# The second layer's front computed by image pairs in program order, attention's rows repeated by the transfer, and two sets of weights built beside the first layer

## Chip, core and metric

The kernel runs on one core of a Trainium2 chip. Time is device time in microseconds (us); lower is better. The kernel before takes 5074.72 us, the median of three runs (5069.09 to 5077.64). The profiled execution is a further run, of 5081.34 us; every position in the text, such as "at 4302.1", is a time in us from the start of its span of 5079.4 us.

The engines are TensorE (PE; its weight loads are shown as PEld), VectorE (DVE), ScalarE (ACT), GpSimd (POOL) and SyncE (SP). SP and ACT issue the transfers (DMA).

## What is computed

The input x has 4 images of 48 x 48 positions with 128 channels, in fp32. There are two layers, each of the form x + f(group_norm(x)).

- Layer 0 is a state-space block: projection to 256 channels, a 3 x 3 convolution, and four scans over the 2304 positions (rows and columns, both ways) with 16 states each; then a normalisation, a gate and a projection back.
- Layer 1 takes the result as 4 sequences of T = 48 frames, each frame a plane of H = 48 by W = 128. It is cut here to what the text needs:

```python
xa_n = inorm(x.reshape(B * T, 1, H, W))           # each frame normalised over its plane
q, k, v = (fno(xa_n, w, ws) for w, ws in (Q, K, V))   # 32 heads each
scores = einsum('bhtd,bhsd->bhts', q, k) / sqrt(d)
out = einsum('bhts,bhsd->bhtd', softmax(scores), v)
attention = inorm(fno(out, wP, wPs) + x)
m = fno(fno(inorm(attention), wM0), wM1)          # with norms and gelu
result = inorm(m) + attention
```

Here `fno(x, w, ws)` is a product by complex weights on the low frequencies of the plane's two-dimensional Fourier transform, transformed back, plus a scaled copy of x.

## The kernel before

**Layouts.** Channels (which are W in layer 1) lie on the 128 partitions. The first layer writes its result `x1` to DRAM as [image, 128, 48, 48]. In the second layer `xa` holds all four images as [128, H = 48, BT = 192], the 192 columns being image by frame. A *pair* is two images, 96 columns. In the second half of the layer the two pairs run as two strands.

**Layer 0 (`layer0`, L54 to 618).** For each of 4 images, 4 directions (in the order 0, 2, 1, 3), 5 chunks of 480 or 384 positions and 16 states there is one step, 1280 in all. The order is written out by hand: operations called through `on` (the class `Ordered`, L36) keep program order on their engine. In a step ACT makes the decay `da` (two activations), VectorE and GpSimd make the input `db`, VectorE runs the scan `h`, GpSimd multiplies `hc` by the row `cbc`, and PE adds up. SP fetches `cbc` and `bbc`, one DRAM row into all 128 partitions, for each group of steps (L425, L429). Work of the background is written as generators in the list `later`; `piece()` (L529) advances one of them by one `yield` per step. The generator `front` (L258) for the next image is put into `later` in the middle of an image's first direction; the last image has no such generator. `back` (L343) writes finished chunks of x1.

**Layer 1's front (`layer1`, L644 on).** Operations here that are called directly on an engine are put in order by the framework's scheduler, not by the program text. The stages are:

- `xa` is loaded from x1, one image at a time by SP and ACT in turn.
- group norm: ACT copies blocks of 8 rows (L993), VectorE takes `bn_stats` of them (L994), `group_affine` (L621) turns means and variances into a scale and a shift per channel and image, and four VectorE operations apply it to `xa` (L1000).
- `first_norm` (L696): the mean of each frame by 48 matmuls with a matrix `mean_m` of constants (L700), subtraction by VectorE and GpSimd (L707), squares by ACT (L709), their mean by another 48 matmuls (L711), and the reciprocal root r.
- `spectral_weights` (L949 to 980): the MLP's two sets of weights are put between Fourier matrices. GpSimd scales `ih` by a weight into `wih` (L972), PE multiplies (L977), ACT copies the result into `spw`, a single buffer (L979), and SP stores it to `sp_d` (L980). There are 16 rounds.
- `prepare` (L824 to 947): selection matrices, and the Q and K weights read with about 140 small transfers each set into its place, and their products `g_qk`.
- V and P weights: their products `gw`, transposed by PE, copied by ACT to `gtt` (L791), and stored by SP to `dgt` (L792) with each of 32 heads repeated 16 times.
- `forward_w` (L722): the transform along W by 48 matmuls (L730); VectorE multiplies by r while it evacuates PSUM (L731), SP stores to `da_x` (L734), and `load_a2` (L737) reads it back turned as `a2`.
- 96 transposes `pxn` (L1024) and their scaled copies `xnt` by ACT (L1027), and 192 matmuls `psel` that select rows of the spectrum (L1042).
- `gp_qk` is a copy of `g_qk` (L1109); with it the scores start.

**Attention.** Scores, softmax and the transposed weights `attn_c` come from L1110 to 1168. Then follow constants `wpv` and `mask` (L1194 to 1203) and the chunk loop (L1220 to 1277): 2 pairs x 4 k x 3 q = 24 steps. In each, `xrep` (1.18 MB, rows of `dxt` repeated 8 times) is loaded with 16 transfers of 16 rows (L1228). At q = 0, four `grep` tiles of 128 rows are loaded from `dgt` (L1236). ACT copies part of `grep` to `gp` (L1243), VectorE multiplies `v` (L1245), GpSimd multiplies `v3` (L1249), and 48 matmuls per step add to `acc` (L1253). At the end of each k the sums become `zt`, which PE transposes as `pz` (L1264 to 1274).

**The rest.** `Strand` has phases p0 to p5 (L1342 to 1700) for the projection back, the norms and the MLP, with the weights `sp_m` read from `sp_d`.

Transfers that SP or ACT issues take one of eight completions per queue in rotation, so that a transfer waits until the one eight places before it in its queue has landed.

Of the kernel before, what the change touches and what calls it, by code (L numbers as in the profile page):

```python
# [53 lines left out]
def layer0(ctx, tc, io, x1_dram):  # L54
# [8 lines left out]
    const = ctx.enter_context(tc.tile_pool(name="l0_const", bufs=1))  # L63
    one = ctx.enter_context(tc.tile_pool(name="l0_one", bufs=1))
# [4 lines left out]
    small = ctx.enter_context(tc.tile_pool(name="l0_small", bufs=2))  # L69
    ps_s = ctx.enter_context(tc.tile_pool(name="l0_pss", bufs=1, space=PSUM))  # L70
    ps_b = ctx.enter_context(tc.tile_pool(name="l0_psb", bufs=1, space=PSUM))
    ps_a = ctx.enter_context(tc.tile_pool(name="l0_psa", bufs=1, space=PSUM))
# [207 lines left out]

    def load_dt(b, k):
        w_dt = two.tile([32 + R, D], F32, tag="w_dt", name=f"w_dt{b}_{k}")
        nc.sync.dma_start(w_dt[32 : 32 + R], io["dt_proj_wT"][k])
        return w_dt
# [58 lines left out]
    def back(b, s, n, yb, x, w, wb):  # L343
# [46 lines left out]
        nc.sync.dma_start(x1_dram[b].rearrange("w h t -> w (h t)")[:, s : s + n], xo[:, 0:n])  # L390
# [196 lines left out]
    for j, chunks in enumerate(directions):  # L587
# [9 lines left out]
        for m, c in enumerate(chunks):  # L597
            c.carry = carries[j % 2]
            for i in range(N):
                if k == ORDER[0] and b + 1 < B and m > 1 and coming is None and not any(g in later for g in backs):  # L600
                    coming = front(b + 1, images[b + 1])
                    later.append(coming)
                if i in (N // 2 + 3, N // 2 + 6):
# [13 lines left out]
    while later:  # L617
        piece()

# [24 lines left out]
def layer1(ctx, tc, io, x1_dram, out):  # L644
# [5 lines left out]
    nc = tc.nc  # L650
    img = ctx.enter_context(tc.tile_pool(name="l1_img", bufs=1))
    const = ctx.enter_context(tc.tile_pool(name="l1_const", bufs=1))
    small = ctx.enter_context(tc.tile_pool(name="l1_small", bufs=2))
    dram = ctx.enter_context(tc.tile_pool(name="l1_dram", bufs=1, space=DRAM))
    dmas = [nc.sync, nc.scalar]
# [6 lines left out]
    def everywhere(name, src, n):  # L662
        return load(name, [128, n], src.partition_broadcast(128), nc.scalar)

    ident = load("ident1", [128, 128], io["c_ident"])
    gmat = load("gmat1", [128, 128], io["c_group"])
    fw = load("fw", [128, 66], io["c_FW"])
    fh = load("fh", [96, 96], io["c_FH"])
    fhi = load("fhi", [96, 96], io["c_FHI"])
    ih = load("ih", [96, 96], io["c_IH"])  # L670
    eps = const.tile([128, 1], F32, name="eps1")
    nc.gpsimd.memset(eps, 1e-5)
    mean_m = const.tile([128, 128], F32, name="mean_m")
    nc.gpsimd.memset(mean_m, 1.0 / (H * W))
    n_g = everywhere("n_g", io["L1_norm_g"], 6)
# [3 lines left out]

    turn = [0]  # L680

    def either():
        turn[0] += 1
        return nc.gpsimd if turn[0] % 3 == 0 else nc.vector
# [8 lines left out]
    def per_image(t, n=HB):  # L693
        return t[:, None, :].to_broadcast([128, n, BT])

    def first_norm(psum, work, x):  # L696

        pm = psum.tile([128, 512], F32, tag="st", name="pm_in")
        for q in range(H // 2):
            nc.tensor.matmul(pm[:, 0 : 2 * BT], mean_m, x[:, 2 * q : 2 * q + 2], start=(q == 0), stop=(q == H // 2 - 1))  # L700
        m = small.tile([128, BT], F32, tag="in_m", name="in_m")
        nc.scalar.copy(m, pm[:, 0:BT])
        nc.vector.tensor_add(m, m, pm[:, BT : 2 * BT])
        pv = psum.tile([128, 512], F32, tag="st", name="pv_in")
        for q in range(0, H, HB):
            d = x[:, q : q + HB]
            either().tensor_sub(d, d, per_image(m))  # L707
            sq = work.tile([128, HB, BT], F32, tag="blk", name=f"sq_{q}")
            nc.scalar.activation(sq, d, AF.Square)  # L709
            for j in range(0, HB, 2):  # L710
                nc.tensor.matmul(  # L711
                    pv[:, 0 : 2 * BT], mean_m, sq[:, j : j + 2], start=(q + j == 0), stop=(q + j == H - 2)
                )
        r = small.tile([128, BT], F32, tag="in_r", name="in_r")
        nc.scalar.copy(r, pv[:, 0:BT])
        nc.vector.tensor_add(r, r, pv[:, BT : 2 * BT])
        nc.scalar.activation(r, r, AF.Sqrt, bias=eps)
        nc.vector.reciprocal(r, r)
        nc.vector.tensor_scalar(r, r, n_g[:, 0:1], None, ALU.mult)
        return r  # L720

    def forward_w(psum, work, src, r, name):  # L722


        da = dram.tile([2, 33, H, BT], F32, name=f"da_{name}")
        for q in range(0, H, HB):
            a = work.tile([66, HB, BT], F32, tag="blk", name=f"a_{name}{q}")
            for j in range(0, HB, 2):
                p = psum.tile([128, 512], F32, tag="mm", name=f"pa_{name}{q}_{j}")
                nc.tensor.matmul(p[0:66, 0 : 2 * BT], fw, src[:, q + j : q + j + 2], start=True, stop=True)  # L730
                nc.vector.tensor_mul(  # L731
                    a[:, j : j + 2], p[0:66, 0 : 2 * BT].rearrange("p (a t) -> p a t", t=BT), per_image(r, 2)[0:66]
                )
            nc.sync.dma_start(da.rearrange("c k h t -> (c k) h t")[:, q : q + HB], a)  # L734
        return da

    def load_a2(a2, da, n):  # L737
        for c in range(2):
            for i, s in enumerate(range(0, n, 11)):
                e = min(s + 11, n)  # L740
                dmas[i % 2].dma_start(a2[c * 48 : (c + 1) * 48, s:e], da[c, s:e].rearrange("k h t -> h k t"))

    xa = img.tile([128, H, BT], F32, name="xa")
    for b in range(B):
        dmas[b % 2].dma_start(xa[:, :, b * T : (b + 1) * T], x1_dram[b])

    pair_t = [img.tile([128, H, 128], F32, tag=f"p{p}", name=f"xnt{p}") for p in range(2)]
    sp_d = [dram.tile([96, 32, 96], F32, name=f"sp_d{i}") for i in range(2)]
# [4 lines left out]
    dgt = dram.tile([4, NH, 16, 3 * NC], F32, name="dgt")  # L753
    with ExitStack() as pw:
        ps_t = pw.enter_context(tc.tile_pool(name="l1_wt", bufs=2, space=PSUM))
        q1 = pw.enter_context(tc.tile_pool(name="l1_w1", bufs=1))

        w_p = q1.tile([128, 12, 2, NH], F32, name="w_p")
        w_v = q1.tile([128, 6, 2, NH], F32, name="w_v")
        d48 = [q1.tile([128, 128], F32, name=f"d48{c}") for c in range(2)]  # L760
        for c in range(2):
            dmas[c].dma_start(w_p[:, :, c], io["wP"][c].rearrange("(j p) h -> p j h", p=128))
            dmas[c].dma_start(w_v[:, :, c], io["wV"][c].rearrange("(j p) h -> p j h", p=128))
            dmas[c].dma_start(d48[c], io[("c_D48r", "c_D48i")[c]])
        for c in range(2):
            p = ps_t.tile([128, 512], F32, tag="tr", name=f"pv48{c}")
            nc.tensor.matmul(p[:, 0:NH], d48[c], w_v[:, 0, c], start=True, stop=True)
            nc.scalar.copy(w_v[:, 0, c], p[:, 0:NH])
# [55 lines left out]
    def prepare():  # L824
# [36 lines left out]
        with ExitStack() as pw:  # L861
# [21 lines left out]
            def weights(side, name, ws, gen, zero, mirror):  # L883
# [5 lines left out]
                for c in range(2):  # L889
# [6 lines left out]
                    for o, r, m in zero:  # L896
                        nc.sync.dma_start(w[o : o + m, 0, c], row[r : r + m])
# [935 lines left out]
```

## Time and profile before

| | |
|---|---|
| median of three runs | 5074.72 us (5069.09 to 5077.64) |
| profiled execution, its span | 5081.34 us, 5079.4 us |
| busy in the span | PE 4207.3, DVE 4169.1, POOL 4034.6, ACT 2923.0 us |
| layer 0, from the start to the last add on x1 | 4200.2 us |
| from there to `gp_qk` | 206.6 us (to 4406.8) |
| scores, softmax, `wpv`, `mask`, `pa0` | to 4543.8 |
| chunk loop | to 4809.4 |
| strands' phases | from 4814.3 to the end |
| layer 0's directions in images 0 to 2 | 260.3, 240.6, 245.4, 265 us |
| the same in image 3 | 249.5, 237.3, 239.5, 262.1 us |

How to read the lines: a line of the *windows* has, for each stretch of time, the busy time and number of instructions of each engine, the granted PE clock (1.00 is full), the share of the DMA engines' time and GB/s. A line of the *chain* has the start, the length and what it was; the chain is followed back from the last instruction to what released each one. A line of the *timeline* has start, length, engine, operation, output and inputs with their shapes, the count, and in brackets the idle time before it and what ended it. A line of the *waits* has who waited for what, the total, the count and the longest.

### The profile page before, as it was taken

To read this page: it belongs to the slowest core of one execution; us is meant where nothing else is said; L and a number is where in the kernel's file an instruction comes from. 1 tells how busy PE (TensorE), PEld (TensorE's weight loads), DVE (VectorE), ACT (ScalarE), POOL (GpSimd) and SP (SyncE) were. 2 spreads that over 40 slices of the span, in tenths; PEclk is the share of its full clock that TensorE was granted. 3 is DMA by queue.
4 is the path that set the end of the run, shared out by engine and by line. 5 is a ranking of instruction groups with operands and counts; after the bars stand their busy time and mean duration, and the time that the engine had idled before them with its cause. 6 is when DMAs were issued, how large, how long until landed. Compare 5 with 4: busy or idle time off the path is not lost. (4 is left out here: it accounts for less than half of the span.)

```text
span 5079.4 us, 44364 instructions
## 1 busy us (share of the span) xinstructions
PE 4207.3 (83%) x12344; PEld 1893.5 (37%) x12344; DVE 4169.1 (82%) x2888; ACT 2923.0 (58%) x6467; POOL 4034.6 (79%) x2219
## 2 busy tenths in 40 slices
PE   6889898888798988887989888878787785888876
PEld 2334333333343333333433333333333332453343
DVE  3689998989899989898999898999999873356636
ACT  3566566666565666665656666656666652223334
POOL 4589998988899989888999898999999873246532
PEclk9989999999899999998999999999999987889977
DMA  1223232322233323222333232333332216236646
GB/s 54 73 88 101 92 114 92 101 88 98 94 106 105 106 91 101 88 98 94 106 103 107 91 102 88 97 105 106 100 103 92 97 66 131 59 82 171 162 106 153
DMA packets 276766, 509.25 MB, mean 100 GB/s; under 512 B 100602, under 2 KB 185434, under 8 KB 276326
## 3 DMA queue, kind: packets, MB, share of 16 engines
q1 hardware_dynamic: 265318, 502.61, 32.5%
q10 hardware_dynamic: 11200, 3.81, 0.5%
q8 instruction: 97, 1.59, 0.1%
q14 instruction: 151, 1.24, 0.1%
HBM read 462.58 MB, written 43.72 MB: 100 GB/s over the span
## 5 line engine op out<-in xcount | busy, mean ns | idle before, releaser
L50 POOL TENSOR_TENSOR hc<-h,cbc 128x960 f32<-128x960 f32 (+1 forms) x1280 | 2719.7, 2140 | 449.2 <-DVE h L50 338.4
L50 DVE TENSOR_TENSOR_SCAN h<-da,carry,db 128x961 f32<-128x961 f32 (+1 forms) x1280 | 2702.4, 2129 | 153.8 <-ACT carry L50 106.0
L50 ACT ACTIVATE da<-dt,a_neg 128x480 f32<-128x480 f32 (+1 forms) x2560 | 1661.3, 649 | 1233.9 <-DVE h L50 1189.3
L50 PE MATMUL yp<-hc,ident 128*128 128x480 f32 (+1 forms) x5120 | 2273.9, 572 | 6.6 <-POOL hc L50 6.4
L50 PEld LDWEIGHTS yp<-hc,ident 128*128 128x128 f32 x5120 | 1006.3, 198 | 1409.7 <-issue 1018.9
L50 DVE TENSOR_TENSOR db<-du,pb 128x960 f32<-128x960 f32 (+1 forms) x960 | 1063.8, 1108 | 232.2 <-PE pb L50 176.8
L50 POOL TENSOR_TENSOR db<-du,bbc 128x960 f32<-128x960 f32 (+1 forms) x320 | 688.6, 2152 | 0.0
L50 PE MATMUL pb<-bs,pick 112*128 112x480 bf16 (+1 forms) x960 | 359.2, 374 | 391.3 <-DVE db L50 389.9
L50 PE MATMUL pc<-pad,cdiag 128*128 128x480 f32 (+1 forms) x630 | 284.6, 564 | 9.0 <-ACT pad L50 9.0
L1249 POOL TENSOR_TENSOR v<-grep,xrep 128x768 f32<-128x768 f32 x96 | 174.1, 1820 | 115.9 <-PE acc L1253 57.7
L1253 PE MATMUL acc<-v,attn_c 128*64 128x384 f32 x1152 | 214.8, 514 | 28.0 <-POOL v L1249 17.8
L1245 DVE TENSOR_TENSOR v<-gp,xrep 128x1536 f32<-128x1536 f32 x96 | 165.1, 1754 | 86.8 <-DMA xrep<-dxt 35.2
L50 POOL TENSOR_TENSOR du<-dt,xc 128x480 f32<-128x480 f32 (+1 forms) x160 | 205.0, 1282 | 37.2 <-ACT dt L50 37.2
L50 ACT COPY db<-carry 128x1 f32<-128x1 f32 x1280 | 226.7, 177 | 7.5 <-DVE db L50 4.2
L50 PE MATMUL px<-xc,w_xp 128*112 128x480 f32 (+1 forms) x320 | 215.0, 759 | 17.0 <-ACT xc L50 13.3
L50 PEld LDWEIGHTS <-pick 112*128 112x128 bf16 x960 | 97.9, 102 | 335.4 <-issue 311.8
L50 ACT ACT_TABLE_LOAD x147 | 188.6, 1283 | 25.7 <-PE gv_g L50 13.8
L50 PE MATMUL pd<-xd,w_dt 8*128 8x480 f32 (+1 forms) x320 | 167.6, 604 | 39.3 <-ACT bs L50 24.4
L50 ACT COPY carry<-h 128x2 f32<-128x2 f32 x1024 | 193.2, 189 | 0.0
L50 PEld LDWEIGHTS pc<-pad,cdiag 128*128 128x128 f32 x630 | 122.1, 195 | 142.4 <-issue 114.7
L50 PE MATMUL yp<-y,ident 128*128 128x480 f32 (+1 forms) x240 | 164.6, 815 | 0.2
L1253 PEld LDWEIGHTS acc<-v,attn_c 128*64 128x64 f32 x1152 | 89.8, 142 | 149.2 <-issue 65.8
(366 smaller groups left out, 3128.9 us busy)
## 6 DMA issues: line engine op xcount, KB each, us to landing
cbc<-cd SPq DMA_DIRECT2D x512, 480.0 KB
bbc<-cd SPq DMA_DIRECT2D x256, 240.0 KB
cbc<-cd SPq DMA_DIRECT2D x128, 384.0 KB
xrep<-dxt SPq DMA_DIRECT2D x384, 72.0 KB
grep<-dgt SPq DMA_DIRECT2D x32, 576.0 KB
bbc<-cd SPq DMA_DIRECT2D x64, 192.0 KB
dgt<-gtt SPq DMA_DIRECT2D x4, 2304.0 KB
x<-in_xT SPq DMA_DIRECT2D x16, 288.0 KB
```

What stands on the lines that cost most here:

```text
L50: return lambda *args, **kw: self._tc.keep_in_program_order(emit(*args, **kw))
L1245: nc.vector.tensor_mul(v, gp[:, None, :, 0:NC].to_broadcast([128, 2, 2, NC]), x[:, :, 0:2])
L1249: nc.gpsimd.tensor_mul(v3, r[:, 2:3].to_broadcast([128, 2, NC]), x[:, :, 2])
L1253: nc.tensor.matmul(acc[c][64 * b : 64 * b + 64, 0:NC], attn_c[:, 2 * pair + b, g, q], v[:, b, c] if c < 2 else v3[:, b], start=first, stop ...
```

## The change

1. The first layer becomes `first_layer`, called from within `layer1`, after DRAM tiles for `sp_d`, `d_w` and `d_m` are made. In its last image a new generator, `matrices`, is put into `later` where other images have `front`. It writes the Q and K weights in their places into DRAM (`d_w`, `d_m`) by about 150 small transfers, and computes `sp_d` with ACT's scaling in place of GpSimd's, in the buffer of `cdiag`, which is idle in that image.
2. The second layer's pools of images, constants and small tiles lie on the other side of the memory. x1 is loaded by pairs into `x_in` ([128, 2, H, T]). Only the last chunk of the last image is stored and loaded by ACT's queue; all others go by SP, and come in program order ahead of it.
3. The front runs through `on`, pair by pair, with the two generators `first_norm` and `forward_w` interleaved. Statistics are taken on `x_in` directly. The group norm's scale goes into the Fourier matrix (`fwa`) and into the vectors of the means (`a_m`), its shift into small corrections. One operation normalises and subtracts the mean. The sums over frames use 32 output columns, in four column groups. r is applied to `a2` after it is loaded, and the Fourier mean is subtracted there. Evacuation goes to VectorE and ACT in turn. The products of V and P weights come after both pairs, and those of Q and K (`products`) after `a2`.
4. `dgt` has each head once. `xrep` and `grep` are filled with one transfer per image or tile that repeats its rows; partitions of `xrep`, `grep`, `attn_c`, `wpv` and `mask` are now ordered (key, head) instead of (head, key).
5. `ih` is loaded just before the strands.

The core of the diff:

```diff
+    def matrices():
+        room = one.tile([128, 9, 128], F32, tag="cdiag", name="matrices")
...
+        for of in range(2):
+            nc.sync.dma_start(
+                d_w[of].rearrange("p c j h -> p (c j) h"), zero[:, None].to_broadcast([128, 8, NH])
+            )
+            nc.sync.dma_start(d_m[of], zero[0:32, None].to_broadcast([32, 2, NH]))
+        yield FREE
...
+                for o, r, m in general + [(at_8, 8, 4)]:
+                    for j in range(4):
+                        k = int(j == 0)
+                        nc.sync.dma_start(dst[j][k:, o : o + m], src[j][k:, r : r + m])
+                    yield FREE
...
+        for n in range(2):
+            for k in range(0, 32, 2):
+                for c in range(2):
+                    for i in range(2):
+                        on.scalar.activation(m[3 + 2 * c + i], m[2], AF.Copy, scale=w[:, n, c, k + i : k + i + 1])
+                    if c == 0:
+                        yield FREE
...
+                on.scalar.copy(room[:, 7 * 96 : 9 * 96], p[0:96, 0:192])
+                nc.sync.dma_start(
+                    sp_dram[n][:, k : k + 2].rearrange("p k m -> p (k m)"), room[:, 7 * 96 : 9 * 96]
+                )
+                yield FREE
...
+                if k == ORDER[0] and b + 1 == B and m > 1 and coming is None and not any(g in later for g in backs):
+                    coming = matrices()
+                    later.append(coming)
...
+    def statistics(psum, p, x):
+        mv = small.tile([128, 2, 2], F32, tag=f"mv{p}", name=f"mv{p}", bufs=1)
+        for b in range(2):
+            st = small.tile([128, 6, 6], F32, tag="st", name=f"st1_{p}_{b}")
+            for q in range(6):
+                on.vector.bn_stats(st[:, q], x[:, b, q * HB : (q + 1) * HB].rearrange("p h t -> p (h t)"))
...
+    def forward_w(psum, work, p, x, aff):
...
+                on.tensor.matmul(pa[0:66, 0 : HB * T], fwa[:, b], x[:, b, q : q + HB], start=True, stop=True)
...
+            nc.scalar.dma_start(
+                da.rearrange("c k h t -> (c k) h t")[:, q : q + HB], a.rearrange("p h b t -> p h (b t)")
+            )
+            yield
...
+    def first_norm(psum, work, p, x, aff, y):
...
+                on.tensor.matmul(
+                    pm[32 * i : 32 * i + 32, 0 : HB * T],
+                    a_m[:, b : b + 1].to_broadcast([128, 32]),
+                    x[:, b, h + q : h + q + HB],
...
+            on.vector.scalar_tensor_tensor(
+                d,
+                x[:, b, h : h + 24],
+                aff[:, 0, b : b + 1],
+                m[:, b, None, :].to_broadcast([128, 24, T]),
+                ALU.mult,
+                ALU.add,
+            )
...
-        spectral_weights(psum, work)
...
+        for p in range(2):
+            aff = statistics(psst, p, x_in[p])
+            norm = first_norm(psst, work, p, x_in[p], aff, xa)
+            trans = forward_w(psum, work, p, x_in[p], aff)
+            next(norm)
+            next(trans)
+            next(norm)
+            for _ in range(5):
+                next(trans)
+                next(norm)
...
+            for s, e in ((0, 17), (17, 33)):
+                v = a2p[:, s:e]
+                on.vector.tensor_mul(v, v, rs[p][0:96, None, :].to_broadcast([96, e - s, 96]))
...
-                        for i in range(8):
-                            nc.sync.dma_start(
-                                x[16 * i : 16 * i + 16, b].rearrange("p c n -> p (c n)"),
-                                dxt[2 * pair + b, k, q * 16 : q * 16 + 16],
-                            )
+                        nc.sync.dma_start(
+                            x[:, b].rearrange("p c n -> p (c n)"),
+                            dxt[2 * pair + b, k, q * 16 : q * 16 + 16][:, None].to_broadcast([16, 8, 3 * NC]),
+                        )
...
-                                dgt[k, 8 * g : 8 * g + 8].rearrange("h r n -> (h r) n"),
+                                dgt[k, 8 * g : 8 * g + 8][None].to_broadcast([16, 8, 3 * NC]),
```

## The prediction

> **What bounds the kernel now.** I read the slices first, then the windows from 4150 us on, the chain of waits there, single lines of the timeline, the transfers of one stretch, and last SyncE's waits.
>
> The page: its span, and VectorE and GpSimd in 40 slices of 127 us.
>
> ```profile
> span 5079.4 us, 44364 instructions
> DVE  3689998989899989898999898999999873356636
> POOL 4589998988899989888999898999999873246532
> ```
>
> Both are near 9 up to slice 33: layer 0, 1280 steps of about 3.25 us, is theirs. It ends at 4200.2 (last add). In the rest no engine is full: chains of waits decide. Windows there (columns: busy us of PE, weight loads, DVE, ACT, POOL; clock; DMA share; GB/s):
>
> ```profile
> 4250.00:4300.00 50.00, 35.94 (x98) 20.18 (x98) 20.50 (x16) 11.09 (x11) 9.96 (x3) 0.86 0.68 138
> 4300.00:4350.00 50.00, 36.46 (x80) 12.64 (x81) 13.68 (x49) 7.53 (x17) 17.93 (x22) 0.82 0.23 66
> 4350.00:4400.00 50.00, 41.91 (x401) 24.41 (x402) 6.84 (x14) 23.05 (x51) 0.00 (x0) 0.81 0.39 79
> 4600.00:4800.00 200.00, 165.61 (x900) 70.24 (x898) 131.17 (x89) 63.78 (x88) 127.69 (x71) 0.95 0.66 173
> ```
>
> The chain through the front (start, length, what):
>
> ```profile
> 4253.16 5.66 DVE xa L1000 x4
> 4258.87 18.07 PE pm_in L700 x48
> ...
> 4285.94 13.18 PE pv_in L711 x40
> ...
> 4303.29 1.89 DMA sp_d<-spw
> 4305.26 0.48 ACT spw L979
> 4305.76 1.87 DMA sp_d<-spw
> ...
> 4363.26 12.62 DMA a_x<-da_x
> ...
> 4387.58 9.46 PE psel L1042 x158
> ...
> 4406.80 0.49 ACT gp_qk L1109
> ```
>
> One engine at a time. The row statistics r are ready at 4302.1, but the transform that needs them starts only here, behind the spectral weights:
>
> ```profile
> 4332.92 0.86 PE L730 MATMUL pa_x<-xa,fw 128*66 128x384 f32 x2 [0.85 <-ACT spw L979]
> ```
>
> So 30.8 us go to 15 rounds of copy 0.48 + store 1.89 through one `spw` buffer, 2.45 us each. From the last add to `gp_qk`, which opens the scores, the front lasts 4406.8 - 4200.2 = 206.6 us.
>
> In attention's chunk loop the chain alternates with transfers:
>
> ```profile
> 4569.65 8.45 DMA grep<-dgt
> 4578.47 0.42 SPq L1228
> ...
> 4581.71 2.62 DMA xrep<-dxt
> ...
> 4605.03 5.92 DMA grep<-dgt
> ```
>
> and the transfers of 4600 to 4645 (GB/s in 40 slices) have two rates:
>
> ```profile
> GB/s 135 143 328 430 340 397 242 381 220 135 86 184 139 180 16 0 0 66 152 183 70 53 148 152 176 148 160 152 176 152 135 152 143 287 410 406 414 303 352 193
> grep<-dgt SPq DMA_DIRECT2D x8, 576.0 KB
> xrep<-dxt SPq DMA_DIRECT2D x57, 72.0 KB
> ```
>
> Near 400 with the 576 KB `grep`, near 150 with the 72 KB `xrep`, which is their issue interval: 72 KB / 0.46 us = 160 GB/s. The first k, loaded ahead, takes 27.9 us (4543.8 to 4571.7); the other seven take 34.0 on average, to 4809.4.
>
> **What the Trainium skill says.** "SBUF — State Buffer", Door 1: DMA bandwidth depends on how many of 16 ports the partitions reach; by its formula 16 rows reach 4 (estimate), 128 all. "DMA: Bandwidth & Descriptors", Rules for kernel authors: coalesce transfers under 64 KB, and issuing from several engines buys no bandwidth. The trace agrees in direction (150 against 400 GB/s), though issue alone explains the 150. "TensorE: Matmul & The Clock Gate", Part 3: matmuls with 32 output columns on different column tiles run together, 2.38 times as fast for three. The trace shows the like in `psel` (0.06 us a pass of 192 columns).
>
> **The change, part by part**, against the profiled run (5081.3 us, span 5079.4; its median of runs 5074.7 is 6.6 lower).
>
> *Front.* `x_in` lands before the last add, since its loads now wait only for buffers freed at about 4172; before, loads were issued 4207 to 4218.8 and the statistics began at 4219. Now VectorE, in program order:
> - pair 0's statistics, 12 bn_stats of 0.5 and a group affine of about 5: 4200.2 to 4211.5.
> - pair 0's norm: `pm` 12 passes x 0.376 (pm_in's 18.06/48) = 4.5; reduction and spreading about 3; four fused normalise passes of 1.26 with six evacuations of 0.5 between, 8; Square and 12 passes of `pv` behind the last, 2.5; second spreading, root with a 1.28 table load, reciprocal, 5; and 12 passes of forward_w, 0.43 each, part of them in between. About 26: 4237.
> - pair 1 the same behind it, 10.4 + 27.3: 4275. Its `da_x` lands at about 4272.
> - dgt's weights behind the norms: VectorE 7, twelve `gtt` copies of 0.47, to 4289.5. The second half of `a_x` queues on SP behind the four dgt stores: 4293.5. Four multiplications by r, 1.7: 4295.
> - 24 `xnt` copies of 0.69 on ACT: 4290 to 4307. psel starts about 4308; before, psel start to gp_qk took 4406.8 - 4383.2 = 23.6. So gp_qk at 4331.6: **-75** (ends -55 and -90). The products of Q and K weights are ready at 4314 with two loads where there were about 140, and hide behind psel.
>
> Column tiling is the unknown here: taken as no gain (18 us for all `pm` and `pv` passes); at 2.38 it saves up to 10.
>
> *Scores and mask.* Two xt copies come earlier, -3; wpv and mask take 11 transfers for 24, -2. The rest of the scores is unchanged.
>
> *Chunk loop.* 384 `xrep` transfers become 48, 6.7 us of issue a step becomes 0.9. dgt is read from one copy; every `cbc` of layer 0 already reads one row into 128 partitions, 480 KB in about 4 us, so I cost repetition at nothing. 5.9 MB per k at 400 GB/s is 15 us, under PE's 24.5 (3 x 8.18). Lower end: the first k's 27.9 for all, 7 x 6.1 = -43; upper end: `grep`'s wait at each boundary stays and PE's clock, 0.95, falls under denser work, -5. I take 30.5 us, 7 x 3.5 = **-24**.
>
> *Last stage.* `ih` loads on SP before `sp_m`: +1.6. The strands' phases after 4814 keep their instructions and their order: 0.
>
> *Layer 0.* The last image takes `matrices`: about 150 small SP transfers and 32 stores, 132 scalings of 96 columns and 34 copies on ACT, 66 matmuls, no VectorE, four tiny GpSimd operations. "ScalarE: Activation LUTs", What ACT_TABLE_LOAD costs, prices an ACTIVATE with a pointer operand at 280 ns + 0.833 a column: 0.36 us, 132 of them 48 (estimate; its 186 ns for a plain copy agrees with 177 for `carry`). Two per step, 0.7, fit into ACT's idle time ahead of `da`, 1233.9/1280 = 0.96 us a step. Without that cover they would hold every scan: about +45. SyncE's cover is
>
> ```profile
> SPq L425 <- POOL hc L50: 2976.7, 637, 19.0
> ```
>
> 4.7 us in each 6.5 us between `cbc` fetches, and a `cbc` has some 12 us in hand (5 steps less landing). Images 0 to 2 with `front` take 19.6 us more than image 3 without; that has 15 us of VectorE and GpSimd, `matrices` almost none: a third, **+7** (ends 0, as it only adds, and +30). The last x1 store and its load go to ACT; behind them wait ACT's first Squares, not due before 4220: nothing.
>
> Sum: -75 - 3 - 2 - 24 + 1.6 + 7 = -95; span 4984, profiled run 4986, median of runs **4980**.
>
> **Rivals.**
> - *The loop gains little* (0.2). `grep` still waits for GpSimd to free its buffers at each k, or PE's clock drops. For: 8.45 and 5.92 are grep's waits. Against: SP was busy with `xrep` just then. It decides if k stays at 34: the -24 falls away, 4980 + 24 = 5004.
> - *The front gains half* (0.14): program order makes pair 1's statistics wait behind pair 0's norm, and `xnt`, psel and `a_x` behind ACT and SP. For: the new chain runs on VectorE alone for 75 us. Against: the 30.8 us of spectral weights and the 19 us of loading are gone in any case. -37 in place of -75: 5018. The change not doing what it says is a part of this case: were `x_in` loaded only after the last store, as before, it would cost 19 of the 75.
> - *More* (0.13): all k at 28 (-19 beyond the forecast's -24) and the column tiles overlap (-10): 4951. For: the first k's 27.9 and psel's 0.06. Against: `grep` fetched for later k has to wait until GpSimd frees its buffer, which it didn't for the first.
> - *Slower* (0.08): SyncE in layer 0. `matrices` puts some 147 transfers ahead of `cbc` fetches in about 28 steps, 91 us. At the 0.3 to 0.37 us that `w` loads took each there is no loss; at 0.75, as under load in the front, 147 x 0.75 - 91 - 12 = +7. They share eight rotating completions, so if each lands late, SP stands: the scans then wait for `cbc`, and at 1.4 us each (landing of 11 us) the loss is 147 x 1.4 - 103 = +103, which with -102 from the other parts is the point of no gain; at 1.6, 5106. For: DRAM to DRAM pieces of 128 bytes appear nowhere in this trace. Against: landings of 2 to 4 us beside the same scans.
>
> **How the numbers follow.** The forecast has 0.43. Two medians of this kernel 0.2% apart (10 us) can't be told apart; its own three runs differ by 0.17%. Faster 0.90 (forecast, loop, half, more), slower 0.08, within 0.2% 0.02, where half a front meets a loss in layer 0. The range leaves out the slower case and the far tail of "more": 4925 to 5035. The forecast's own range is 4955 to 5000.
>
> **What would show it.** Right: last add near 4207; no spw line after it; gp_qk 125 to 145 us after the last add; `xrep` gone from the chain within k; k at 29 to 32 us; image 3's direction 0 within 10 us of 249.5. Wrong: GpSimd's hc or VectorE's scan waiting for `cbc` in image 3 by tens of us; a `po` or `in_r` wait that makes a pair take over 35 us; k still at 34.

## The result and the profile after

The changed kernel takes 5017.89 us, the median of four runs (5017.53 to 5021.33), against 5076.18 us for the kernel before (5069.09 to 5078.46, four runs). The ratio is 0.9889, with a 95% interval of 0.9875 to 0.9903. So 58 us are gained, where 95 were forecast. Its profiled execution has a span of 5016.0 us, 63.4 less than before. The stages account for it:

| stage, us | before | after | change | forecast |
|---|---|---|---|---|
| layer 0, to the last add on x1 | 4200.2 | 4206.6 | +6.4 | +7 |
| front, to the start of `gp_qk` | 206.6 | 132.6 | -74.0 | -75 |
| scores and mask, `gp_qk` to the first `e_w` | 120.5 | 121.9 | +1.4 | -5 |
| `e_w` to the last `pa0` product | 16.3 | 16.2 | -0.1 | 0 |
| chunk loop, from there to the strands' first product | 270.7 | 270.7 | 0 | -24 |
| strands, to the end | 265.1 | 268.0 | +2.9 | +1.6 |

(The last stage took 263 to 269 us in the runs below without a change to it.) Two stages are as forecast, and two are not: the chunk loop and the mask. The lines that answer to those of before follow. First, the page and the windows (columns as before):

```profile
span 5016.0 us, 44268 instructions
DVE  3689998989899989898999898988999985556536
POOL 4589998988899989898999898888999983246531
```

```profile
4250.00:4300.00 50.00, 38.60 (x186) 18.30 (x186) 25.48 (x52) 20.42 (x40) 2.26 (x35) 0.86 0.30 67
4300.00:4350.00 50.00, 46.81 (x545) 29.04 (x544) 20.99 (x52) 21.58 (x56) 8.47 (x5) 0.86 0.05 10
4350.00:4400.00 50.00, 45.97 (x302) 26.17 (x300) 34.26 (x35) 11.00 (x22) 25.07 (x13) 0.93 0.14 32
4550.00:4750.00 200.00, 168.51 (x900) 99.49 (x897) 131.41 (x99) 64.74 (x89) 129.20 (x85) 0.90 0.67 159
```

From 4300 on the front's PE is busy 46.8 of 50 us; before it had 36.5 there, with `spw` waits between. In the loop nothing is better: PE 168.5 in 200 us against 165.6, and 159 GB/s against 173. The chain through the front:

```profile
4217.52 4.07 PE pm L50 x24
...
4229.33 2.12 PE pv L50 x6
...
4244.68 2.78 DVE st L50 x6
...
4280.05 0.76 DVE in_r L50
...
4294.94 8.74 PE pxn L1151 x60
...
4320.52 8.94 PE psel L1169 x158
```

No `spw` and no wait for `a_x` is left on it, and pair 1's statistics start at 4244.7, right behind pair 0's r. The end of the front, in the timeline of ACT:

```profile
4339.22 0.48 ACT L1236 COPY gp_qk<-g_qk 128x384 f32<-128x384 f32 x1
```

The chain at the mask and in the loop:

```profile
4452.23 8.76 DMA mask<-in_c_ident
...
4498.96 9.00 DMA grep<-dgt
...
4520.35 6.66 DMA xrep<-dxt
...
4530.92 9.77 DMA grep<-dgt
```

The 16 issues of `xrep` are gone from it, as forecast, but the transfers themselves wait longer: 9.0 and 9.8 us for `grep` (8.5 and 5.9 before) and 6.7 for `xrep` (2.6). The transfers from 4535 to 4580, in 40 slices, show why:

```profile
GB/s 236 250 234 229 254 246 225 250 238 234 250 119 12 0 0 0 0 53 303 238 233 213 8 15 49 283 234 229 246 234 254 229 238 250 217 254 242 221 254 246
```

One rate now, near 240 GB/s, in place of 400 for `grep` and 150 for `xrep`. `xrep` has gained and `grep` has lost. At the loop's start and at each k's end two images of `xrep` and four tiles of `grep` are wanted together, and the sum is as late as it was. Counted from the last `pa0` product to the second `zt` of each k, the first k takes 34.5 us (28.8 before), the next six 33 to 34 (32 to 35). The last one, behind which no `grep` is left to load, takes 27.5 (32.7).

Layer 0's first direction of the last image, where the small transfers of `matrices` run, takes 263.7 us (249.5 before); the other three take 238.2, 239.2 and 261.0 (237.3, 239.5, 262.1). Some 4 us are won back behind the last scan: from there to the last add it is 31.7 us (35.7 before).

### The profile page after: what moved, and what is told of

Read it like the earlier page. It is cut to its first block, busy times and chain, and to the rows that moved or that the text cites. A ratio compares the mean times of both kernels' runs of the same rounds, so it can differ in the third digit from the quotient of the medians.

```text
span 5016.0 us, 44268 instructions
## 1 busy us (share of the span) xinstructions
PE 4181.6 (83%) x12444; PEld 1916.5 (38%) x12444; DVE 4170.1 (83%) x2901; ACT 2953.2 (59%) x6608; POOL 3993.4 (80%) x2188
## 4 chain that ended last, share of the span: by engine, by line
DVE 17%; PE 15%; ACT 7%; issue 7%; POOL 3%; DMA 3%; SPq 1%; DVEq 0%; POOLq 0%; ACTq 0%
DVE h L50 12%; PE yp L50 4%; ACT da L50 3%; DVE db L50 3%; PE acc L1381 2%; POOL v L1377 1%; DMA grep<-dgt 1%; ACT L50 1%; PE sc L1254 1%; PE pi_p L50 1%; POOL db L50 1%; ACT dt L50 1%; POOL hc L50 1%; DVE m L50 1%; PE pe_m L50 0%
## 5 line engine op out<-in xcount | busy, mean ns | idle before, releaser
L1381 PE MATMUL acc<-v,attn_c 128*64 128x384 f32 x1152 | 218.2, 513 | 36.5 <-ACT s L1389 32.1
L1371 ACT COPY gp<-grep 128x768 f32<-128x768 f32 x96 | 77.0, 803 | 157.3 <-DVE v L1373 79.7
```

The lines of the kernel that those rows point to most:

```text
L1371: nc.scalar.copy(gp[:, :, 0:NC], r[:, 0:2])
L1381: nc.tensor.matmul(acc[c][64 * b : 64 * b + 64, 0:NC], attn_c[:, 2 * pair + b, g, q], v[:, b, c] if c < 2 else v3[:, b], start=first, stop ...
```

## The experiments

Each run up to the one on the spectral weights is a single execution. The kernel before, on the same chip, took 5065.94 us beside the first two, the copies and the third buffer, 5067.97 us beside the halves (median of nine), and 5076.31 us beside the others. Times of stages are read from each run's own trace.

**Which property of the new transfers makes them slow?** Three theories: the form of 16 by 8 rows; the repetition of rows; or that PE, its clock and GpSimd set the loop whatever the transfers do.

```diff
-    dxt[2 * pair + b, k, q * 16 : q * 16 + 16][:, None].to_broadcast([16, 8, 3 * NC]),
+    dxt[2 * pair + b].rearrange("k (u s) n -> (k u) s n", s=12)[:, 0:8],
-    dgt[k, 8 * g : 8 * g + 8][None].to_broadcast([16, 8, 3 * NC]),
+    dxt[g].rearrange("k (u s) n -> (k u) s n", s=12)[:, 0:8],
```

> The changed kernel, but xrep and grep are filled with 128 rows that are all different (taken from dxt at 16 places of 8 rows with a gap between the places), in the same form of 16 by 8 rows and the same sizes; the attention's products are therefore made from other rows than the reference's. Measured in the changed kernel: loads of repeated rows move at about 240 GB/s, the chunk loop from 4477.7 to 4747.9 takes 270 us up to the strand's first pass. Theory shape (a transfer of 16 by 8 rows is dealt to the 16 engines so that they hinder each other at the partitions): still about 240 GB/s, loop 265 to 275 us. Theory repetition (reading the same row 8 or 16 times is slow): near 400 GB/s, loop 235 to 250 us. Theory engines (PE, its clock and GpSimd set the loop): rate may change, loop stays at 265 to 275 us.

Measured: 5019.39 us, loop 274.0 us, and the transfers from 4535 to 4580:

```profile
GB/s 213 246 228 225 217 242 229 233 250 217 250 209 250 98 16 0 0 0 0 0 66 254 225 238 233 33 15 74 266 217 258 229 229 242 221 217 238 229 229 238
```

Rows that are all different are no faster. Repetition is out. The second run takes different rows in the plain form:

```diff
-    dxt[2 * pair + b, k, q * 16 : q * 16 + 16][:, None].to_broadcast([16, 8, 3 * NC]),
+    dxt[2 * pair + b].rearrange("k s n -> (k s) n")[0:128],
-    dgt[k, 8 * g : 8 * g + 8][None].to_broadcast([16, 8, 3 * NC]),
+    dxt[g].rearrange("k s n -> (k s) n")[0:128],
```

> The changed kernel, but xrep and grep are filled with 128 different rows that lie one after the other, as one plain transfer of 128 rows; the attention's products are again made from other rows than the reference's. Theory shape: near 400 GB/s in bursts, loop 235 to 250 us. Theory repetition: the same. Theory engines: near 400 GB/s, loop stays at 265 to 275 us.

Measured: 4989.60 us, loop 247.0 us, periods of 29.1 to 31.8 us, and from 4500 to 4545:

```profile
GB/s 242 377 385 266 324 352 373 213 84 0 0 0 0 57 315 414 262 0 0 7 164 426 414 410 197 281 373 385 369 320 389 356 115 12 0 0 0 0 0 0
```

The same bytes in the same buffers move at up to 426 GB/s, and the loop is 23.7 us shorter, which is the -24 of the forecast. (The last period is 27.2 us.) So PE, its clock and GpSimd do not set the loop, and it is the form of the transfer that costs. One difference is left between the two forms: the plain rows lie in one piece in DRAM, those of the 16 by 8 form in 16 pieces. No run separates these two; `cbc`, which reads one row again and again in the plain form, reaches 399 GB/s in the kernel before (2028 to 2048, in slices of 0.5 us), so a source in one piece is not needed for a high rate.

A later run cut these plain transfers in two halves of 64 partitions:

```diff
-    x[:, b].rearrange("p c n -> p (c n)"), dxt[2 * pair + b].rearrange("k s n -> (k s) n")[0:128],
+    for u in range(0, 128, 64):
+        x[u : u + 64, b].rearrange("p c n -> p (c n)"),
+        dxt[2 * pair + b].rearrange("k s n -> (k s) n")[u : u + 64],
```

(and `grep` alike)

> As the run with 128 different rows in one plain transfer (bursts near 400 GB/s, loop 247.0 us), but each of these transfers is cut into two plain ones of 64 partitions; again other rows than the reference's. Theory partitions (64 neighbouring partitions reach 8 of the 16 ports that the Trainium skill's SBUF page describes, so that two engines share one, as with 16 by 8 rows): 200 to 250 GB/s, loop 262 to 276. Theory form (three-dimensional descriptions of a transfer are slow as such): near 400 GB/s, loop 245 to 250.

Measured: 5004.11 us, loop 259.2 us, and from 4500 to 4545:

```profile
GB/s 229 234 234 225 229 229 229 238 225 234 240 217 229 229 180 180 311 205 238 135 4 0 0 0 7 0 0 115 283 238 213 250 221 240 221 234 217 242 221 238
```

The rate is as the theory of partitions said, though the loop was a little better than its 262. A transfer need not have three dimensions to be slow: a plain one to half of the partitions is as slow as 16 by 8 rows. That the 16 by 8 form is slow for the same reason does not follow from it. What the two have in common the windows show (columns as before; changed kernel, run with 128 plain rows, run with halves):

```profile
4564.00:4580.00 16.00, 10.22 (x52) 4.50 (x49) 9.11 (x8) 3.73 (x6) 8.61 (x5) 0.82 1.03 238
4523.70:4527.00 3.30, 3.30 (x24) 1.97 (x22) 2.94 (x3) 0.80 (x1) 3.19 (x2) 1.00 1.02 415
4532.00:4545.00 13.00, 10.03 (x64) 4.77 (x62) 8.33 (x8) 3.74 (x6) 8.26 (x5) 1.00 1.03 230
```

The DMA engines' share is full in all three. So the slow forms leave no engine idle and do not wait for SP's issues: each row simply takes longer, 0.32 us for 4.6 KB against 0.18 (worked out from share and rate for 16 engines).

For the halves this fits the Trainium skill: "SBUF — State Buffer", Door 1, says that bandwidth depends on how many of 16 ports the partitions reach, and that 64 partitions reach 8; here 230 GB/s against 415. For 16 by 8 rows that rule is not enough, since together they reach all 128 partitions. "DMA: Bandwidth & Descriptors", The descriptor swizzle, says that a plain transfer of 128 partitions gives each engine one port. If the 16 by 8 form gives engine r the partitions 8r to 8r + 7, these are two ports, both shared with another engine (an estimate from the page's formula). No run here shows how either form is dealt to the engines; that step stays argued.

**Can copies or buffers repair it?** First, copies of dgt in DRAM and `grep` in the plain form:

```diff
+        for k in range(4):
+            for g in range(4):
+                nc.sync.dma_start(dg16[k, g], dgt[k, 8 * g : 8 * g + 8][None].to_broadcast([16, 8, 3 * NC]))
         products()
...
-                                dgt[k, 8 * g : 8 * g + 8][None].to_broadcast([16, 8, 3 * NC]),
+                                dg16[k, g].rearrange("r h n -> (r h) n"),
```

> The changed kernel, but dgt is copied 16 times from DRAM to DRAM while the scores run (16 transfers on SP behind the loads of a2), and grep is loaded from the copies as one plain transfer of 128 rows, as before the change; xrep stays as changed. Late loads (shape or repetition): grep near 400 GB/s, the waits of 9.0 and 9.8 us for grep at each k fall to 3 to 5, loop 270 to 240 to 255 us; the mask, which queues behind the first grep, lands some 4 us sooner. Theory engines: loop 265 to 275. The copies cost nothing if hidden in the scores (DMA share 0.05 to 0.24 there), up to 25 us if the a2 or dxt transfers queue behind them.

Measured: 5006.67 us. The loop takes 258.5 us, just above the range; `gp_qk` comes 3.9 us later and the mask does not land sooner (scores 123.8). In the chain the `grep` wait at the first k's end has gone, and waits of 6.8 to 7.8 us are left at the next three. Then a third `xrep` buffer:

```diff
-  tag="xrep", name=f"xrep{pair}_{k}_{q}")
+  tag="xrep", name=f"xrep{pair}_{k}_{q}", bufs=3)
```

(with single buffers for `s1` and `zt`)

> The changed kernel with three xrep buffers in place of two (paid for by single buffers for s1 and zt); loads as changed. If the loop waits for loads because they start too late (two buffers) though 5.9 MB per k at 240 GB/s is 24.6 us of 33: the burst at each k loses the 1.2 MB of xrep that is then already there, loop 245 to 258 us. If the four grep buffers alone set the start of the burst: 260 to 270 us. Theory engines: 265 to 275 us.

Measured: 5021.19 us, loop 274.2 us. Nothing is gained. By its number this is the theory of the engines, but the run with plain rows has ruled that out, and in the loop the chain now waits for `grep` alone:

```profile
4503.84 10.31 DMA grep<-dgt
...
4532.48 10.95 DMA grep<-dgt
```

So the four `grep` buffers set the burst: in the code they come free only in the last q of a k.

**The mask.** wpv and mask become constants:

```diff
+    wpv = const.tile([128, 2, 4], F32, name="wpv")
+    mask = const.tile([128, 3, T], F32, name="mask")
...
-        wpv = p1.tile([128, 2, 4], F32, name="wpv")
-        mask = p1.tile([128, 3, T], F32, name="mask")
```

(their loads go along)

> The changed kernel, but wpv and mask lie in the pool of constants and are loaded with the second layer's other constants, ahead of the front. In the changed kernel 11 issues of 0.6 us and 8.8 us for the last mask transfer, which lands behind the first grep and xrep loads, stand between the last dxt store (4446) and e_w (4461.1). Theory: from gp_qk to e_w 121.9 falls by 10 to 15 us, to 107 to 112, the rest unchanged, span 5001 to 5006. Rival (the first xrep or grep load, which is itself slow, sets the start of the loop anyway): e_w earlier, but the end of the loop moves by less than 5 us.

Measured: 5013.69 us, span 5011.9. From `gp_qk` to the first `e_w` 106.6 us, 15.3 less; but the last `pa0` product comes only 7.7 us sooner after `gp_qk`, since it now waits for the softmax, and then `xrep` is waited for, 7.6 us. Against the changed kernel the span falls by 4.1. Theory and rival were each half right: the mask was late by 15 us, and about half of that had cover. What it waited for in the changed kernel is in the transfers from 4448.5 to 4456.5:

```profile
GB/s 1 1 0 0 1 0 0 0 0 0 0 0 0 1 0 0 0 0 0 1 1 0 0 0 0 1 1 0 0 0 0 0 0 0 0 0 0 0 0 0
DMA packets 832, 0.00 MB, mean 0 GB/s; under 512 B 832, under 2 KB 832, under 8 KB 832
```

For 8 us nothing but tiny packets moves. They are those of the eight `wpv` loads ahead of the mask in SP's queue, which put one number of 4 bytes into each of 128 partitions: 1024 pieces, about 100 in a us. Only behind them do the mask's rows move, together with two `grep` tiles issued after it.

**Layer 0.** The small transfers are left out:

```diff
-                        nc.sync.dma_start(dst[j][k:, o : o + m], src[j][k:, r : r + m])
+                        pass
```

(and those of `d_w`'s first rows and of `d_m`)

> The changed kernel without the 136 small transfers from DRAM to DRAM in matrices (its four fills with zeros stay, so that Q and K weights are zero and the output is not the reference's); the scalings, products and stores of the spectral weights in layer 0 stay. In the changed kernel the last image's first direction takes 263.7 us against 249.5 before, and the other three 0.5 us less than before. Theory SyncE (the pieces, 0.6 us each, delay cbc and bbc): first direction back to 249 to 252, last scan at 4160 to 4164, span 5001 to 5006. Rival ACT (the scalings delay da): the first direction falls by less than 5 us, or the spectral work, now earlier, makes it 255 or more.

Measured: 5009.80 us, last scan at 4163.7 (4174.9 with the pieces), the image's directions 249.4, 237.4, 239.6 and 262.1 us, those of the kernel before within 0.2. So the 132 scalings, the products and the 32 stores cost nothing, and the pieces cost all 14 us. In the changed kernel's trace they are these, and from 3317 to 3440 GpSimd waited for what stood behind them (first the transfers by tile, then the waits; neither wait is there in the kernel before, nor in this run):

```profile
L306 SPq DMA_DIRECT2D d_w<-in_wQ x32: 583/620/847, 3321.0 to 3379.6; - x32
L306 SPq DMA_DIRECT2D d_w<-in_wK x32: 591/604/776, 3393.3 to 3436.0; - x32
```

```profile
POOL db L50 <- DMA bbc<-cd: 9.6, 1, 9.6
...
POOL db L50 <- DMA d_w<-in_wK: 5.7, 1, 5.7
```

They hold SP for about 0.6 us each. The row that `db` reads, and that came late, is `bbc`, not `cbc`.

**Part 4 undone**, in the changed kernel: transfers, order of rows and the 16 stored copies as before.

```diff
-                nc.sync.dma_start(dgt[k], gt.rearrange("h c n -> h (c n)"))
+                nc.sync.dma_start(
+                    dgt[k], gt.rearrange("h c n -> h (c n)")[:, None].to_broadcast([NH, 16, 3 * NC])
+                )
...
+                        for i in range(8):
+                            nc.sync.dma_start(
+                                x[16 * i : 16 * i + 16, b].rearrange("p c n -> p (c n)"),
+                                dxt[2 * pair + b, k, q * 16 : q * 16 + 16],
+                            )
```

> The changed kernel with part 4 undone: order (head, key), 16 transfers of 16 rows for each xrep, dgt stored 16 times by SP ahead of the loads of a2, grep as a plain transfer of 128 rows, wpv and mask by 24 transfers. Theory (the old loop lost to issue what the new one loses to the slow form of transfer): loop 268 to 274 as before and after; mask 3 to 6 us faster than in the changed kernel; gp_qk 12 to 22 us later, since 9.4 MB stand before the second half of a2. Span 5020 to 5035, so that part 4 is worth some 10 to 15 us by its single dgt store alone. Rival (part 4 gains in the loop and loses elsewhere): loop 280 or more.

Measured: 5044.23 us. The loop takes 267.8 us and the scores 119.0: both 3 us better than in the changed kernel. But `gp_qk` comes 36.0 us later (34.1 of them between the last add and `gp_qk`), more than expected:

```profile
4296.12 43.35 DMA dgt<-gtt
```

VectorE waits 40.7 us for the last quarter of `a_x` there. So part 4 is worth about 26 us, all of it through the smaller dgt that no longer stands on SP ahead of `a_x`; in the loop and the mask it costs some 6. It also means that the front's 74 us are not the pairs' alone: with the old dgt in the new order the front took 166.7 us, 40 less than before.

**Was moving the spectral weights within the front enough?** In the kernel before:

```diff
-        spectral_weights(psum, work)
         mv = small.tile([128, B, 2], F32, tag="mv", name="mv1")
...
         nc.scalar.copy(u32, pu[0:24, 0:BT])
+        spectral_weights(psum, work)
```

> The kernel before, with one call moved: spectral_weights stands behind the selection of the spectrum in the program text, so that the scheduler gives the front's transforms the first place; nothing else is changed. Theory (15 rounds of the spw buffer between r and the first transform cost the front 30.8 us of its 74): gp_qk 25 to 31 us earlier, at 4376 to 4382, and the span shorter by 20 to 31 us, less what the 16 rounds take from PE in the scores (32 us of matmuls). Rival (the transforms would have waited for something else, as the loads of constants or PE): gp_qk earlier by less than 12 us.

Measured: 5080.68 us; `gp_qk` at 4406.0, where it was (4406.8). The rival's number came (less than 12 us), but not for its reason. The chain shows the 16 rounds in their new place, and the selection of the spectrum begun 35 us sooner (4347.9 for 4383.2):

```profile
4351.78 6.69 PE psel L1041 x158
...
4370.88 0.47 ACT spw L979
4371.36 1.85 DMA sp_d<-spw
4373.31 0.48 ACT spw L979
```

The transforms did wait for nothing else, but ACT and PSUM are shared with what follows, so that the rounds held `ps` and `gp_qk` instead: PE's first `ps` stands at 4400.4, right behind an `spw` copy. So it does not help to move them within the front; in layer 0, as the run without the pieces shows, they cost nothing.

**All findings together.** The first try had the copies of dgt behind `products()`, five `grep` buffers, wpv and mask as constants, and the small transfers two or four to a step:

```diff
-    pg = ph.enter_context(tc.tile_pool(name="l1_qg", bufs=4))
+    pg = ph.enter_context(tc.tile_pool(name="l1_qg", bufs=5))
...
                         nc.sync.dma_start(dst[j][k:, o : o + m], src[j][k:, r : r + m])
-                    yield FREE
+                        if j % 2:
+                            yield FREE
```

> The changed kernel with the findings put together: dgt copied 16 times in DRAM behind the products of Q and K weights and grep loaded as plain transfers with five buffers; wpv and mask loaded with the constants; the small transfers of matrices two or four to a step instead of four to ten. Sum of the single runs: layer 0 4 to 10 us less, mask and start of the loop 6 to 8 less, loop 12 to 18 less, the copies 0 to 3 more: 20 to 33 us under the changed kernel, median 4985 to 4998. Rival (the pieces cost the same however they are spread, and the loop's start waits for the slow xrep): 5000 to 5006.

Measured: 5049.15 us (median of five; ratio to before 0.9960, 0.9947 to 0.9974), a miss: each k behind the first took 28.2 to 30.9 us, but the loop began more than 100 us late (its first product stood 106 us behind the last of `pa0`). I put that down to a `grep` load ahead of the `dxt` stores on SP, gave `dxt`, `grep` and `xrep` the program's order there, and moved the copies to the start of the scores (cut):

```diff
+        for name in ("tensor", "vector", "scalar", "gpsimd", "sync"):
...
-                    nc.sync.dma_start(dxt[b, k], xt.rearrange("r c n -> r (c n)"))
+                    on.sync.dma_start(dxt[b, k], xt.rearrange("r c n -> r (c n)"))
```

> The combined kernel with its fault taken out: there SP issued a grep load ahead of the dxt stores, and it stood 98 us for a buffer that the scores still used, so that the loop began 118 us late; within the loop each k took 28.2 to 30.9 us. Now dxt, grep and xrep transfers keep program order on SP, and the copies of dgt are issued behind the front, at the start of the scores. Theory (the parts add up): last add 12 to 16 us earlier than in the changed kernel, e_w 10 to 15 earlier in the scores, loop 240 to 250 against 270.7: span 4968 to 4985, median 4970 to 4988. Rival (the copies hold the front or the dxt stores, or the first xrep sets the start of the loop): 4990 to 5005.

Measured: 5077.97 us (median of 21; 1.0012, 1.0005 to 1.0018). The reading was wrong. Its chain shows `xt` and `dxt` in turn, each alone, once the scores are over:

```profile
4447.46 2.60 DMA dxt<-xt
4450.68 1.53 PE pxt L1238 x8
4453.85 2.59 DMA dxt<-xt
```

In both kernels 15 of GpSimd's 16 `xt` sums stand behind the scores, from 4445 us on. My reading is that the framework's scheduler put them there because it reckons with the copies ahead of the `dxt` stores in SP's queue. The next run puts the copies back ahead of `products()` and changes nothing else against the first try:

```diff
+        for k in range(4):
+            for g in range(4):
+                nc.sync.dma_start(dg16[k, g], dgt[k, 8 * g : 8 * g + 8][None].to_broadcast([16, 8, 3 * NC]))
         products()
-        for k in range(4):
-            for g in range(4):
-                nc.sync.dma_start(dg16[k, g], dgt[k, 8 * g : 8 * g + 8][None].to_broadcast([16, 8, 3 * NC]))
```

> The combined kernel again, with the copies of dgt back ahead of the products of Q and K weights (as in the run with copies alone), since behind them the scheduler put 15 of the 16 xt sums after the scores (GpSimd's first waited 123 us), so that each xt, dxt round ran alone, 6.4 us each. Here the xt sums stand between the score products again. mask early, small transfers spread, five grep buffers as in the two combined kernels. Theory (the parts add up once the order is kept): last scan at 4153 to 4158, gp_qk 4328 to 4336, e_w 105 to 110 behind it, loop 240 to 255: span 4967 to 4990, median 4970 to 4992. Rival (the five buffers make the first xrep or the dxt stores wait again, or the copies hold the front): 5000 or more.

Measured: 4974.29 us (median of five), a ratio of 0.9808 to the kernel before (0.9794 to 0.9821), so it beats both; the sums stand among the scores again. Its span of 4969.6 us is 46.4 under the changed kernel's: layer 0 -12.2 (the last image's first direction takes 249.4 us), front +4.5, `gp_qk` to the last `pa0` product -5.9, loop -29.3 (241.4 us), strands -3.5. How much the fifth `grep` buffer has in this was not measured alone. On the chain a wait of 6.8 us for `xrep` is left at the loop's start and waits of 6.6 to 9.1 us for `grep` at six of the k, so the loop is not at its end.

## Why the prediction was right where it was, and wrong where it was not

**Range and sign** held: 5018 lies in 4925 to 5035, outside the forecast's own 4955 to 5000. It is also the number of the rival in which the front gains half, but the front gained all. The case that came is the rival in which the loop gains little, at 5004; a mask that did not gain its 5 us but lost 1.4, and 1.3 us more in the strands, bring it to 5012. The rest is the step from the span to the median: the profiled run of before lay 6.6 us over its median, and I took that off, but the changed kernel's lies at its median. Its mechanism was only half named. GpSimd's late release of `grep` is real, as the third `xrep` buffer showed. PE's clock did fall in the loop (0.90 from 0.95 in the windows shown), but over the whole loop with plain rows it was 0.94, under denser work; the rate of the transfers was the reason.

**Front**, -74.0 for -75. Pair 0 took 11.0 us for its statistics (11.3 forecast) and 27 for its norm (26), pair 1 9.5 and 27 (10.4 and 27.3); psel began at 4313.8, 107 us after the last add (108). The sum is right in part by luck. I priced a pass of `pm` as 18.06/48, but 48 is the count of records, and an fp32 matmul leaves two of them: in the code `pm_in` is 24 matmuls. (The other counts of 48 matmuls in the text on the kernel before are records too, and the 192 of `psel` are 96 matmuls; a transpose leaves one record.) The 12 matmuls of `pm` are 24 records, 9.0 us at that price and not 4.5. They took 4.07 us, since the column tiles do run together, which I had taken as no gain: 2.2 times for four tiles, where the Trainium skill, "TensorE: Matmul & The Clock Gate", Part 3, has 2.38 for three. So two errors cancelled. `pv` was not so lucky: its quarters come one by one, three matmuls each on the same column tile, 2.05 us a quarter and 8.2 in all for the 4.5 that I had. forward_w has the same slip: its 12 matmuls took 8.6 us a pair (1.44 for two), where I had 5.2. From the first normalise pass to the end of `pv` it is 15 us, and all but 2.6 of them are PE's on the chain, where I had seen VectorE. What came behind, spreading, root and reciprocal, took 2.5 us for my 5.

**Spectral weights.** That the 30.8 us were a cost of the front is confirmed by the shift of psel by 35 us; that they would come back by being moved a little was not, and I had not claimed it. Layer 0's cover on ACT held: nothing was lost to the scalings.

**Layer 0**, +6.4 for +7, right by its sum and wrong by its place, which is luck. I took a third of what `front` costs, without a mechanism. In fact SP's transfers cost 14 us in one direction, the stretch behind the last scan gave 4 back, the other directions half a us, and the first images were 3 us ahead in this run. My rival on SP had the mechanism, with `cbc` for `bbc`; at the 0.6 us measured its formula, 147 x 0.6 - 103, gave no loss at all, because it lets SP's slack be shared over all 28 steps. The pieces come in bursts, up to 13 one after the other (8.1 us), and a burst meets one fetch.

**Chunk loop**, 0 for -24: the step that failed is "so I cost repetition at nothing", with 400 GB/s for all of the 5.9 MB. The evidence that I drew on, `cbc`'s one row into 128 partitions, was about repetition, and there it was right: different rows were as slow. (Its 480 KB in 4 us are only 120 GB/s to the landing; while they move the rate reaches 399.) It said nothing on the form. `cbc` is a plain transfer over 128 partitions, `xrep` and `grep` had become 16 by 8. At the measured 240 GB/s a k's 5.9 MB take 24.6 us, as long as PE's work, and most of them are asked for at once. The size of the prize was right: with plain transfers the loop is 23.7 us shorter.

**Mask**, +1.4 for -5: I counted transfers, 11 for 24, and not what they are made of. The last one landed 8.8 us after its issue (1.7 before): by the trace its queue first carried the 1024 pieces of `wpv`, for 4.3 us, and then the mask together with two `grep` tiles. The pieces were as many before, but SP and ACT shared them, with the mask's parts in between. With the fast `grep` of the run with copies the mask came no sooner: the same tiny packets are all that moves from 4454.5 to 4462 there. Why so small a piece takes as long as it does stays open.

## What to carry to other kernels

Fewer transfers are not faster ones: before merging many small transfers into one, look at what form the merged one has on the partition side, and take its rate from a transfer of that very form in a trace. Count the pieces too: eight transfers of 128 numbers held up the mask for 8 us. When a stage's loads are bound by rate or by the time a buffer comes free, ask first which buffer is released last; a further buffer elsewhere buys nothing. Work put into a hidden place hides only as finely as it is cut: the same small transfers cost 14 us in bursts and none when spread over more steps.

## What was unexpected of the hardware

- Transfers of 576 KB in the form of 16 by 8 rows move at 230 to 240 GB/s, with equal or with different rows; the same bytes as 128 plain rows at up to 426; plain halves of 64 partitions at about 230. The DMA engines are busy all the while in each.
- A piece of DRAM to DRAM of a few rows holds SP for 0.6 us beside the scans, against 0.3 to 0.5 for a fetch of 480 KB.
- Loads of one 4-byte number per partition moved about 100 packets in a us (832 in 8 us) with nothing else in flight.
- Four column tiles of 32 outputs together took 0.17 us a record of 384 columns, against 0.376 for one of 128 outputs; three matmuls in turn on one column tile took 0.34 a record.
